# A feature-interaction network on one core: where fc's columns come from, the dummy products of the start, and the queues that load W0 and W1

## The chip, the cores and the metric

The kernel runs on one core of a Trainium2 chip. A core has a matrix engine (TensorE, PE in the profile), a vector engine (VectorE, DVE), a scalar engine (ScalarE, ACT), a general engine (GpSimd, POOL) and an engine that mostly starts transfers (SyncE, SP). Transfers are started from the queues of SP, ACT and POOL, and sixteen DMA engines carry them out. The metric is the device time of one execution in microseconds (us); lower is better. Three runs of the kernel before took 737.26, 740.76 and 745.29 us, median 740.76.

## The reference

The input `x` holds 1,024 samples, 39 fields and 64 values each, in float32. Three layers follow each other, each a sum over all products of a field of the layer's input with a field of `x`:

```python
F, E, HID = 39, 64, [64, 64, 64]
def _cin_layer(Xk, X0, W, b):
    Wr = W.reshape(O, Hk, Fdim)
    return jnp.einsum('bhe,bfe,ohf->boe', Xk, X0, Wr) + b[None, :, None]
Xk = X0
for W, b in ((W0, b0), (W1, b1), (W2, b2)):
    Xk = _cin_layer(Xk, X0, W, b)
    outs.append(Xk.sum(axis=-1))
return jnp.concatenate(outs, axis=-1) @ fc_w.T + fc_b
```

`fc_w` is one row of 192 numbers, 64 for each layer. The result is one number per sample.

## The kernel before, in words

The last step takes only sums over the 64 values and a weighted sum over the channels. So the kernel folds layers 2 and 3 and the output row into weights once, at its start, and then does the two products that remain over all samples.

**The start (the `prep` part, the first 20 us).** From W2 and the third part of `fc_w` it makes V2, a 64 x 39 matrix (line 400, tile `pv`; two DVE transposes at line 417; copies into tile `v2`, lines 427 and 428). The second part of `fc_w` becomes the fortieth column of V2 (`v2[..., F:FT]`, line 424). W0 is transposed on PE (line 411, `pw`) and copied into the upper half of `both` (line 448). V2 times W1 (line 452, tiles `pt` and `pv`) is copied into `part` (line 463), transposed on PE (line 472) and copied into the lower half of `both` (line 481). From `both`, small additions on DVE and copies on ACT (`weight_rows`, lines 498 and 500) make `pairs`, weights for products of two fields, which PE turns into `wa` (`weight_turn`, lines 517 to 519), chunk by chunk.

**The fc columns.** `fc_w` comes as a row into one partition (`fcrow`, line 243, SP). A column of 64 numbers, one a partition, is made on PE as a product of the row with the number one (line 351, `turn_row`, five of them; line 353 for the third part, which is needed twice with a mask by the parity of the partition, lines 311, 332 to 335 and 356). They lie in the PSUM bank `small` and are copied by ACT to `v2` (line 424), `fc` and `fc0s` (lines 645 to 647).

**Dummies.** `spin` (line 277) issues products of ones into the bank `idle`; nobody reads it. Every float32 product shows as two records in the profile.

**The table of products.** Fields are gathered by index from DRAM tables: `gather_rows` (line 171) on POOL fills the tiles `rt`, `ut`, `vt`. The first gathers read `xh`, two transposed pieces of `x` that ACT's queue loads (line 247); SP copies `xh` into the table `xd` (line 390), which later gathers read. DVE multiplies two gathered tiles (`product`, line 211), PE multiplies the result with `wa` (`multiply`, line 533, and `join`, lines 553 and 564), ACT and DVE finish (lines 581, 583, 594).

**Order.** The order on each engine is the program's own, written by hand. The first loads are issued on ACT's queue one behind another: W2, the first `xh`, W0's two halves (line 253), W1's two halves (line 257), the second `xh`. [...]

**The main loop.** 32 blocks of 2,048 columns, in pairs: 13 chunks a pair, each four products of 128 x 512 on PE, save the seventh, which `join` takes.

Of the kernel before, what the change touches and what calls it, by code (L numbers as in the profile page):

```python
# [75 lines left out]
MM = 512  # L76
# [4 lines left out]
NW = 20  # L81
# [63 lines left out]
def cin_kernel(ctx: ExitStack, tc: tile.TileContext, x, w0t, b0, w1, b1, w2, b2, fc_w, fc_b, out):  # L145
    nc = tc.nc
# [13 lines left out]
    def bank(name):  # L160
        return psum.tile([128, MM], F32, name=name, tag="po")
# [43 lines left out]
    def product(n, c, cols=slice(0, BLK), p=None):  # L205
        if p is None:
            p = prods.tile([128, BLK], F32, name="p", tag="p")
        if c < NPAIR:
            i, k = PAIRS[c]
            r = rt[n % 2]  # L210
            nc.vector.tensor_tensor(p[:, cols], r[:, i, cols], r[:, k, cols], ALU.mult)  # L211
        else:
            nc.vector.tensor_tensor(p[:, 0:SUB], ut[n // 2 % 2], vt[n // 2 % 2], ALU.mult)  # L213
        return p

    prep = tc.tile_pool(name="prep", bufs=1)
    with prep as prep:
        w2s = prep.tile([128, FH // 2], F32, name="w2s")
        w1s = prep.tile([128, FH // 2], F32, name="w1s")
        w0s = prep.tile([128, NW * H], F32, name="w0s")  # L220
        part = prep.tile([FT, 4 * NA, H], F32, name="part")
        fcrow = prep.tile([1, 3 * H], F32, name="fcrow")
        fcrow2 = prep.tile([1, H, 2], F32, name="fcrow2")
# [9 lines left out]
        parity = prep.tile([128, 2], I32, name="parity")  # L233
        mask = prep.tile([128, 2], F32, name="mask")

        nc.vector.memset(ones, 1.0)
        nc.vector.memset(fc2, 0.0)
        nc.vector.memset(v2, 0.0)  # L240
        nc.vector.memset(warm, 0.0)
        w0v = w0t.rearrange("b a h -> b (a h)")
        nc.sync.dma_start(fcrow, fc_w)
        nc.scalar.dma_start(w2s, w2.rearrange("o (s n) -> (o s) n", s=2))

        def load_half(k):
            nc.scalar.dma_start(
                xh[k].rearrange("f (b e) -> b f e", e=E), x[k * SB : (k + 1) * SB]
            )

        load_half(0)
        for s, n in enumerate((NW, F - NW)):
            nc.scalar.dma_start(
                w0s[H * s : H * s + F, 0 : n * H], w0v[:, s * NW * H : (s * NW + n) * H]
            )
        for s in range(2):
            nc.scalar.dma_start(
                w1s[H * s : H * s + H], w1[:, s * FH // 2 : (s + 1) * FH // 2]
            )
        load_half(1)  # L260
        nc.gpsimd.iota(place, pattern=[[0, 1]], base=0, channel_multiplier=1)
        for i in range(NT):
            at = OFFSET[i] - 3 * K + (0 if i < NT - 1 else -F)
# [10 lines left out]
        small = bank("small")  # L274


        def spin(n=1, cols=MM // 2):
            for _ in range(n):
                nc.tensor.matmul(  # L279
                    idle[:, 0:cols],  # L280
                    nc.const_aps.tensor(1.0, (128, 128), F32),
                    nc.const_aps.tensor(1.0, (128, cols), F32),
                    start=True,
                    stop=True,
                )

        spin(3)
        spin(1, MM // 4)


# [17 lines left out]

        row, j, f0, late, v, extra = (new() for _ in range(6))
        nc.vector.tensor_copy(row, place)  # L310
        nc.vector.tensor_scalar(parity[:, 1:2], place, 1, None, ALU.bitwise_and)
# [17 lines left out]
        nc.vector.tensor_copy(lists[:, 0:NT], fields_of)  # L329
        nc.vector.tensor_scalar(lists[:, NT : 2 * NT], fields_of, float(FT), None, ALU.add)  # L330

        nc.gpsimd.tensor_copy(mask[:, 1:2], parity[:, 1:2])
        nc.gpsimd.tensor_scalar(mask[:, 0:1], mask[:, 1:2], -1.0, 1.0, ALU.mult, ALU.add)
        for s in range(2):
            nc.gpsimd.tensor_copy(fcrow2[:, :, s], fcrow[:, 2 * H : 3 * H])

        for k, series in enumerate((U_STEPS, V_STEPS)):
            for i, (at, by) in enumerate(series):
                nc.gpsimd.memset(steps_at[:, k, i : i + 1], float(at))
# [5 lines left out]
            nc.gpsimd.dma_start(xd[k][F::FT].rearrange("r (p c) -> p r c", c=128), ones)  # L345


        one = ones[0:1, 0, 0:1]

        def turn_row(dst, k):  # L350
            nc.tensor.matmul(dst, fcrow[:, k * H : k * H + H], one, start=True, stop=True)

        nc.tensor.matmul(
            small[:, 0:1], fcrow2.rearrange("p h s -> p (h s)"), one, start=True, stop=True
        )
        nc.vector.tensor_scalar(fc2[:, 0::32], mask, small[:, 0:1], None, ALU.mult)
        nc.vector.tensor_scalar(unit, apart, 0, None, ALU.is_equal)
        for k in range(3):
            turn_row(small[0:H, k + 1 : k + 2], k)
        for k in range(2):  # L360
            turn_row(small[H:128, k + 4 : k + 5], k)
        spin()


        r, most, seat, far = (new() for _ in range(4))
        both_of = prep.tile([128, 2], F32, name="both_of")
# [30 lines left out]
        for k in range(2):  # L397
            for u in range(2):
# [5 lines left out]
                    start=True,  # L404
                    stop=True,
                )

        for s in range(2):
            for k in range(NW // 2):
                n = min(128, (F - NW * s) * H - k * 128)  # L410
                nc.tensor.transpose(  # L411
                    pw[s][0:n, k * FT : k * FT + F],
                    w0s[H * s : H * s + F, k * 128 : k * 128 + n],
                    unit[H * s : H * s + F, H * s : H * s + F],
                )
# [6 lines left out]
        for s, at in enumerate((2, 5)):  # L422
            rows = slice(H * s, H * s + H)
            nc.scalar.copy(v2[rows, s, F:FT], small[rows, at : at + 1])
# [26 lines left out]
        for k, a in groups:  # L451
# [4 lines left out]
                start=True,  # L456
                stop=True,
# [19 lines left out]
        for k, a in groups:  # L477
            for t in range(2):
                lo = max(NA * k, a + NQ * t)
                n = a + NQ * t + NQ - lo  # L480
# [1 line left out]
                    both[H:128, lo * FT : (lo + n) * FT],  # L482
                    turns[k][H * t : H * t + H, (NQ - n) * FT : NQ * FT],
                )
        spin(4)
        first = [prods.tile([128, BLK], F32, name="p", tag="p") for _ in range(3)]


# [140 lines left out]
    p = {}  # L629
    for k, (n, c) in enumerate(steps[:3]):  # L630
# [28 lines left out]
    for at, (n, c) in enumerate(steps[:-TAIL]):  # L659
# [26 lines left out]
        if at + AHEAD < len(steps):  # L686
            n, c = steps[at + AHEAD]
# [70 lines left out]
```

## Time and profile before

The profiled execution took 737.11 us; its span from the first instruction to the last is 735.3 us.

| what | value |
|---|---|
| median of three runs | 740.76 us |
| profiled execution, span | 737.11 us, 735.3 us |
| PE busy | 729.6 us |
| main products, line 533: 1,536 records | 665.3 us, 593 ns each |
| table products, DVE line 211: 197 | 433.9 us, 2,236 ns each |
| gathers into r, POOL line 171: 156 | 327.1 us, 2,097 ns each |
| dummies, line 279: 22 records | 7.4 us, 484 ns each |
| first record of line 533 | at 19.83 us |

A line of the timeline shows start, busy time, engine, source line, operation, result and inputs, shape and number of records; in brackets stands the idle time before it and what ended it. PE records overlap, so that a record's own duration is longer than the distance to the next. POOL's times are rough.

### The profile page before, as it was taken

The numbers are of one execution on the slowest core, as the hardware profiler recorded it, in microseconds if no ns is written. First come the engines' busy times: TensorE is split into PE (matmuls) and PEld (weight loads), VectorE is DVE, ScalarE is ACT, GpSimd is POOL, SyncE is SP. The second block draws the span as 40 slices with busy tenths as digits, with TensorE's granted clock in tenths as the row PEclk, the third lists the DMA queues.
The fourth block names the chain that finished last, engine by engine and source line by source line (L and its number), as shares of the span: only waits on it lengthen the run. The fifth ranks groups of instructions, "written<-read, shape, count | busy, mean of one in ns | idle before, by whom it ended". The sixth has DMA issues, their size and how long they took to land.

```text
span 735.3 us, 6438 instructions
## 1 busy us (share of the span) xinstructions
PE 729.6 (99%) x2414; PEld 319.1 (43%) x2414; DVE 640.7 (87%) x521; ACT 167.1 (23%) x244; POOL 406.2 (55%) x256
## 2 busy tenths in 40 slices
PE   9999999999999999999999999999999999999998
PEld 6444344444444444444444444444444444444443
DVE  6987998888889888898888889888899888889885
ACT  3232122221212221122221212222122221212222
POOL 7978698547545465554447545465654457545300
PEclk9999999999999999999999999999999999999999
DMA  9869869988576895767878686795767876566700
GB/s 298 335 227 347 329 247 346 386 320 294 233 275 240 301 353 236 262 242 276 321 282 280 235 284 245 297 363 208 270 251 271 330 286 253 221 251 247 285 1 1
DMA packets 63656, 197.25 MB, mean 268 GB/s; under 512 B 37684, under 2 KB 37733, under 8 KB 43656
## 3 DMA queue, kind: packets, MB, share of 16 engines
q0 software_dynamic: 29040, 186.22, 65.6%
q1 hardware_dynamic: 32894, 8.63, 5.1%
q10 hardware_dynamic: 1690, 1.99, 1.1%
q8 instruction: 19, 0.31, 0.2%
q14 instruction: 13, 0.11, 0.0%
HBM read 196.76 MB, written 10.60 MB: 282 GB/s over the span
## 4 chain that ended last, share of the span: by engine, by line
PE 90%; POOL 4%; DVE 2%; DMA 2%; issue 1%; ACT 0%; DVEq 0%
PE po L533 83%; PE po L553 4%; POOL r L171 3%; PE po L564 2%; DMA r<-xd,lists 1%; DMA b0s<-in_b 1%; DVE g L583 1%; DVE p L211 1%; PE pt L452 0%; PE pv L400 0%; POOL v L171 0%; PE pv L452 0%; PE pw L411 0%; POOL u L171 0%; DVE wide L303 0%
## 5 line engine op out<-in xcount | busy, mean ns | idle before, releaser
L533 PE MATMUL po<-p,wa 128*128 128x512 f32 x1536 | 665.3, 593 | 0.8 <-DVE p L211 0.7
L211 DVE TENSOR_TENSOR p<-r 128x2048 f32<-128x2048 f32 (+2 forms) x197 | 433.9, 2236 | 72.0 <-PE po L533 67.0
L171 POOL DMA_INDIRECT r<-xd,lists x156 | 327.1, 2097 | 267.6 <-issue 262.4
L533 PEld LDWEIGHTS po<-p,wa 128*128 128x128 f32 x1536 | 289.8, 190 | 371.6 <-issue 350.0
L581 ACT ACTIVATE z<-po,fc0s 64x512 f32<-64x512 f32 x128 | 87.4, 683 | 378.7 <-PE po L564 216.3
L583 DVE SCALAR_TENSOR_TENSOR g<-po,b0s,z 64x512 f32<-64x512 f32 x128 | 95.9, 749 | 11.5 <-ACT z L581 5.3
L576 ACT COPY g<-r 39x1024 f32<-39x1024 f32 x64 | 66.7, 1043 | 158.9 <-DVE sums L594 122.2
L594 DVE TENSOR_REDUCE sums<-g 103x16 f32<-103x1024 f32 x62 | 75.6, 1220 | 2.1
L171 POOL DMA_INDIRECT u<-xd,lists x16 | 30.6, 1912 | 4.9 <-issue 4.6
L553 PE MATMUL po<-p,wa 32*64 32x512 f32 x512 | 31.6, 600 | 0.0
L171 POOL DMA_INDIRECT v<-xd,lists x16 | 27.9, 1742 | 4.9 <-issue 4.9
L213 DVE TENSOR_TENSOR p<-u,v 128x1024 f32<-128x1024 f32 x16 | 19.5, 1218 | 0.0
L553 PEld LDWEIGHTS po<-p,wa 32*64 32x64 f32 x512 | 9.4, 131 | 20.2 <-issue 19.4
L564 PE MATMUL po<-u,wa 32*64 32x512 f32 x256 | 17.0, 587 | 0.0
L171 POOL DMA_INDIRECT r<-xh,lists x8 | 7.7, 966 | 2.9 <-issue 2.1
L564 PEld LDWEIGHTS po<-u,wa 32*64 32x64 f32 x256 | 5.7, 132 | 8.0 <-issue 8.0
L279 PE MATMUL idle<-const-float32-1.0 128*128 128x256 f32 (+1 forms) x22 | 7.4, 484 | 0.8 <-PEq L745 0.8
L500 DVE TENSOR_TENSOR pairs<-both 128x2 f32<-128x2 f32 (+27 forms) x59 | 6.1, 172 | 0.4 <-issue 0.3
L279 PEld LDWEIGHTS idle<-const-float32-1.0 128*128 128x128 f32 x22 | 5.2, 254 | 1.6 <-issue 0.7
L518 ACT COPY wa<-tr 128x128 f32<-128x128 f32 x8 | 2.1, 266 | 15.1 <-PE tr L517 15.1
L165 POOL DMA_DIRECT2D xd<-in_x x5 | 5.3, 1077 | 0.0
L517 PE MATMUL tr<-unit,pairs 128*128 128x128 f32 x8 | 2.3, 287 | 0.6 <-ACT wa L519 0.5
(101 smaller groups left out, 62.2 us busy)
## 6 DMA issues: line engine op xcount, KB each, us to landing
xd<-in_x SPq DMA_DIRECT2D x26, 312.0 KB
r<-xd,lists POOLq DMA_INDIRECT x156, 8.9
xd<-in_x POOLq DMA_DIRECT2D x5, 312.0 KB, 6.4
w2s<-in_w ACTq DMA_DIRECT2D x1, 624.0 KB
w1s<-in_w ACTq DMA_DIRECT2D x2, 312.0 KB
xh<-in_x ACTq DMA_DIRECT2D x2, 156.0 KB
xd<-xh SPq DMA_DIRECT2D x2, 156.0 KB
u<-xd,lists POOLq DMA_INDIRECT x16, 10.0
```

The costliest lines, as they stand in the source:

```text
L171: nc.gpsimd.indirect_dma_start(dst, None, table, bass.IndirectOffsetOnAxis(ap=lists[:, k : k + 1], axis=0))
L211: nc.vector.tensor_tensor(p[:, cols], r[:, i, cols], r[:, k, cols], ALU.mult)
L213: nc.vector.tensor_tensor(p[:, 0:SUB], ut[n // 2 % 2], vt[n // 2 % 2], ALU.mult)
L279: nc.tensor.matmul(idle[:, 0:cols], nc.const_aps.tensor(1.0, (128, 128), F32), nc.const_aps.tensor(1.0, (128, cols), F32), start=True, sto ...
L500: nc.vector.tensor_tensor(out, diagonal(a, b, sa, sb), diagonal(b, a, sb, sa), ALU.add)
L533: nc.tensor.matmul(po[n][m], wa[:, c, side : side + 2 * H], p[:, bass.ts(m, MM)], start=n % 2 == 0 and c == 0, stop=n % 2 == 1 and c == NP ...
L553: nc.tensor.matmul(dst[half * H : half * H + H], wa[rows, NPAIR, at : at + H], p[rows, bass.ts(side, MM)], start=t >= 2, stop=t < 2 and ha ...
L564: nc.tensor.matmul(dst[half : half + H], wa[rows, NPAIR + 1, H : 2 * H], ut[n // 2 % 2][rows, bass.ts(side, MM)], start=False, stop=t < 2,)
L576: nc.scalar.copy(gt[H : H + F], rt[n % 2][0:F, 0, bass.ts(m, SUB)])
L581: nc.scalar.activation(z[one], po[n][m][other], AF.Identity, bias=fc0s[other])
L583: return lambda: nc.vector.scalar_tensor_tensor(g[n][m // 2][0:H, at], po[n][m][one], b0s[one], z[one], ALU.add, ALU.mult)
L594: nc.vector.tensor_reduce(sums[:, b_at : b_at + SB], g[n][m // 2].rearrange("p (b e) -> p b e", e=E), AX.X, ALU.add,)
```

## The change

It has four parts.

1. `fcrow`, its products, its mask and the bank `small` go. The columns of `fc_w` come by transfers of SP, each of 64 single words (`fc_column`): two into every other partition of `fc2`, two into `v2`, one of three columns into `fc`, two into `fc0s`.
2. The dummies of the start have 2 x 512, 256 and 128 columns instead of 3 x 256 and 128; the one behind the light products goes; 512 and 256 columns are added between the V2 products and the transposes of W0. In front of the first `weight_turn`, `spin(4)` becomes `spin(2, MM)`, the same number of columns.
3. SP loads the first `xh` and the second halves of W0 and W1; ACT loads W2, the first halves and the second `xh`.
4. The clearing of `fc2` comes first on DVE, since the transfers into it wait for it.

```diff
-        nc.sync.dma_start(fcrow, fc_w)
+        def fc_column(dst, k, n=1):
+            nc.sync.dma_start(dst, fc_w[:, k * H : (k + n) * H].rearrange("o (k h) -> h (o k)", h=H))
...
         nc.scalar.dma_start(w2s, w2.rearrange("o (s n) -> (o s) n", s=2))
-        load_half(0)
-        for s, n in enumerate((NW, F - NW)):
-            nc.scalar.dma_start(
+        for s in range(2):
+            fc_column(fc2[s::2, 32 * s : 32 * s + 1], 2)
+        load_half(0, nc.sync)
+        for s, engine in enumerate((nc.scalar, nc.sync)):
+            n = NW - s
+            engine.dma_start(
                 w0s[H * s : H * s + F, 0 : n * H], w0v[:, s * NW * H : (s * NW + n) * H]
             )
+        for s, engine in enumerate((nc.scalar, nc.sync)):
+            engine.dma_start(w1s[H * s : H * s + H], w1[:, s * FH // 2 : (s + 1) * FH // 2])
+        load_half(1, nc.scalar)
         for s in range(2):
-            nc.scalar.dma_start(
-                w1s[H * s : H * s + H], w1[:, s * FH // 2 : (s + 1) * FH // 2]
-            )
-        load_half(1)
+            fc_column(v2[H * s : H * s + H, s, F:FT], 1)
+        fc_column(fc, 0, 3)
+        for s in range(2):
+            fc_column(fc0s[H * s : H * s + H], 0)
...
-        spin(3)
+        spin(2, MM)
+        spin()
         spin(1, MM // 4)
...
-        nc.gpsimd.tensor_copy(mask[:, 1:2], parity[:, 1:2])
-        nc.gpsimd.tensor_scalar(mask[:, 0:1], mask[:, 1:2], -1.0, 1.0, ALU.mult, ALU.add)
-        for s in range(2):
-            nc.gpsimd.tensor_copy(fcrow2[:, :, s], fcrow[:, 2 * H : 3 * H])
...
-        nc.tensor.matmul(
-            small[:, 0:1], fcrow2.rearrange("p h s -> p (h s)"), one, start=True, stop=True
-        )
-        nc.vector.tensor_scalar(fc2[:, 0::32], mask, small[:, 0:1], None, ALU.mult)
         nc.vector.tensor_scalar(unit, apart, 0, None, ALU.is_equal)
-        for k in range(3):
-            turn_row(small[0:H, k + 1 : k + 2], k)
-        for k in range(2):
-            turn_row(small[H:128, k + 4 : k + 5], k)
-        spin()
...
+        spin(1, MM)
+        spin()
         for s in range(2):
             for k in range(NW // 2):
...
-        spin(4)
+        spin(2, MM)
...
-    nc.scalar.copy(fc, small[0:H, 1:4])
-    nc.scalar.copy(fc0s[0:H], small[0:H, 1:2])
-    nc.scalar.copy(fc0s[H:128], small[H:128, 4:5])
```

More of the change, by code (lines that the diff above doesn't have):

```diff
@@ L221, in cin_kernel @@
         part = prep.tile([FT, 4 * NA, H], F32, name="part")
-        fcrow = prep.tile([1, 3 * H], F32, name="fcrow")
-        fcrow2 = prep.tile([1, H, 2], F32, name="fcrow2")
         fc2 = prep.tile([128, H], F32, name="fc2")
@@ L232, in cin_kernel @@
         lane = prep.tile([128, 1], I32, name="lane")
-        parity = prep.tile([128, 2], I32, name="parity")
-        mask = prep.tile([128, 2], F32, name="mask")
+        nc.vector.memset(fc2, 0.0)
         nc.vector.memset(ones, 1.0)
-        nc.vector.memset(fc2, 0.0)
         nc.vector.memset(v2, 0.0)
@@ L242, in cin_kernel, with load_half @@
         w0v = w0t.rearrange("b a h -> b (a h)")
-        nc.sync.dma_start(fcrow, fc_w)
-        nc.scalar.dma_start(w2s, w2.rearrange("o (s n) -> (o s) n", s=2))
-        def load_half(k):
-            nc.scalar.dma_start(
+        def fc_column(dst, k, n=1):
+            nc.sync.dma_start(dst, fc_w[:, k * H : (k + n) * H].rearrange("o (k h) -> h (o k)", h=H))
+        def load_half(k, engine):
+            engine.dma_start(
                 xh[k].rearrange("f (b e) -> b f e", e=E), x[k * SB : (k + 1) * SB]
             )
-        load_half(0)
-        for s, n in enumerate((NW, F - NW)):
-            nc.scalar.dma_start(
+        nc.scalar.dma_start(w2s, w2.rearrange("o (s n) -> (o s) n", s=2))
+        for s in range(2):
[3 more added lines that the diff above has]
+            n = NW - s
+            engine.dma_start(
                 w0s[H * s : H * s + F, 0 : n * H], w0v[:, s * NW * H : (s * NW + n) * H]
             )
+        for s, engine in enumerate((nc.scalar, nc.sync)):
+            engine.dma_start(w1s[H * s : H * s + H], w1[:, s * FH // 2 : (s + 1) * FH // 2])
+        load_half(1, nc.scalar)
         for s in range(2):
-            nc.scalar.dma_start(
-                w1s[H * s : H * s + H], w1[:, s * FH // 2 : (s + 1) * FH // 2]
-            )
-        load_half(1)
+            fc_column(v2[H * s : H * s + H, s, F:FT], 1)
+        fc_column(fc, 0, 3)
+        for s in range(2):
+            fc_column(fc0s[H * s : H * s + H], 0)
         nc.gpsimd.iota(place, pattern=[[0, 1]], base=0, channel_multiplier=1)
@@ L273, in cin_kernel @@
         pw = [bank("pw") for _ in range(2)]
-        small = bank("small")
         def spin(n=1, cols=MM // 2):
@@ L310, in cin_kernel @@
         nc.vector.tensor_copy(row, place)
-        nc.vector.tensor_scalar(parity[:, 1:2], place, 1, None, ALU.bitwise_and)
         step(row, F, 1.0, j)
@@ L345, in cin_kernel @@
             nc.gpsimd.dma_start(xd[k][F::FT].rearrange("r (p c) -> p r c", c=128), ones)
-        one = ones[0:1, 0, 0:1]
-        def turn_row(dst, k):
-            nc.tensor.matmul(dst, fcrow[:, k * H : k * H + H], one, start=True, stop=True)
-        nc.tensor.matmul(
-            small[:, 0:1], fcrow2.rearrange("p h s -> p (h s)"), one, start=True, stop=True
-        )
-        nc.vector.tensor_scalar(fc2[:, 0::32], mask, small[:, 0:1], None, ALU.mult)
-        nc.vector.tensor_scalar(unit, apart, 0, None, ALU.is_equal)
-        for k in range(3):
-            turn_row(small[0:H, k + 1 : k + 2], k)
-        for k in range(2):
-            turn_row(small[H:128, k + 4 : k + 5], k)
-        spin()
+        nc.vector.tensor_scalar(unit, apart, 0, None, ALU.is_equal)
         r, most, seat, far = (new() for _ in range(4))
@@ L421, in cin_kernel @@
         column = blocks.rearrange("h k (f j) -> h (k f) j", j=32)[:, :, 0]
-        for s, at in enumerate((2, 5)):
-            rows = slice(H * s, H * s + H)
-            nc.scalar.copy(v2[rows, s, F:FT], small[rows, at : at + 1])
         for s in range(2):
```

## The prediction

> **What bounds the kernel now.** I read the page first, then the chain of waits from 60 us on, then the PE, POOL and DVE timelines of the first 45 us.
>
> ```profile
> span 735.3 us, 6438 instructions
> PE 729.6 (99%) x2414; PEld 319.1 (43%) x2414; DVE 640.7 (87%) x521; ACT 167.1 (23%) x244; POOL 406.2 (55%) x256
> ```
>
> PE is hardly ever idle (735.3 - 729.6 = 5.7 us). The chain says from when that is true without a break (start, length, what):
>
> ```profile
> 79.10 2.29 DVE p L211
> 81.39 0.04 issue
> 81.44 7.13 PE po L533 x16
> ...
> 91.33 41.40 PE po L533 x96
> ```
>
> From 81.44 us the chain holds PE pieces alone up to 730.36 us. The change touches none of that: the 653.9 us after 81.44 stay. What it can do is to bring the 81.44 us mark forward or push it back. Two things lead to it. PE's own work is one (main products from 19.83 us on); the other is the table gathers on POOL, whose last members DVE waits for (the chain shows a gather landing from 60.74 to 68.94 us, then DVE, then PE at 81.44).
>
> The PE timeline of the start (start, busy, what):
>
> ```profile
> 0.78 3.33 PE L279 MATMUL idle<-const-float32-1.0 128*128 128x256 f32 x8 [0.78 <-PEq L745]
> ...
> 7.07 2.40 PE L400 MATMUL pv<-w2s,fc 128*64 128x320 f32 x8
> 9.40 1.91 PE L411 MATMUL pw<-unit,w0s 39*128 39x39 f32 x20
> 11.24 2.50 PE L452 MATMUL pt<-w1s,v 128*128 128x320 f32 x4
> 13.54 2.17 PE L452 MATMUL pv<-w1s,v 128*128 128x320 f32 x4
> ...
> 17.08 2.01 PE L279 MATMUL idle<-const-float32-1.0 128*128 128x256 f32 x8
> ```
>
> The reader should divide. The eight L452 records take 11.24 to 15.64 us: 550 ns for 320 columns, 1.72 ns a column. The dummies at 17.08 take (19.03 - 17.08)/8 = 244 ns for 256, 0.95 a column; the main products 41.40/96 = 431 ns for 512, 0.84. So until 15.6 us PE ran at half speed. The page's clock row says 9 and the windows 1.00 throughout: that row does not show this state.
>
> [...] DMA share 0.95 to 1.19 in every microsecond from 3 to 20 us. [...]
>
> ```profile
> 17.70 0.94 POOL L171 DMA_INDIRECT r<-xd,lists  x1 [0.30 <-issue]
> ...
> 23.20 5.27 POOL L171 DMA_INDIRECT r<-xd,lists  x1 [0.30 <-issue]
> ```
>
> and on DVE
>
> ```profile
> 22.90 4.63 DVE L211 TENSOR_TENSOR p<-r 128x1024 f32<-128x1024 f32 x4
> ```
>
> The 5.27 us gather ends at 28.47, 0.94 us after the DVE run ended at 27.53. A gather gets its 0.94 us of work done only between DVE products.
>
> **The change, part by part.**
>
> *Dummies (PE).* 2 x 512 + 256 + 128 columns, two records each, 2,816 column-records at 1.72 ns = 4.8 us: from 0.78 to 5.6 us without a gap, where before the dummies stopped at 4.11. [...]
>
> *V2's input.* W2 was there by 4.83 us (the ACT queue's second xh load waits for that semaphore and is issued then). Now 156 KB of xh run beside it: at the window's 380 GB/s, 0.4 us, so 5.2. The two fc2 words' transfers (64 words each) are issued by SP after a DVE memset at about 1.0 and 1.4 us. The trace has such a transfer only under full load: bias and b0s, 0.2 KB, 4.4 and 4.6 us to landing; fcrow, one row, was in use 1.3 us after issue (0.73 to 2.03). Bounds 2.7 and 6.0; I take 3.5, under the dummies. L400 starts at 5.6 instead of 7.07 and takes 1.2 (released) to 2.3 us. DVE must first end its index lists (7.03 us before, less 0.4 for parity and the fc2 product): its two transposes and copies then run 6.7 to 8.4 (or to 9.2, if L400 is slow), against 8.45 to 10.52. The 768 dummy columns behind L400 (1.5 us at 0.95) end near 8.3, under that cover. The 20 W0 transposes at L472's released rate, 1.44/20 = 72 ns, take 1.4 instead of 1.8: to 9.7.
>
> *L452.* It needs v2 (9.2 at the latest), both halves of W1 and now v2's fc words. In the program's order of waits, the second half of W1 [...]must wait for the semaphore of W2's load: issued at 5.2 instead of 3.64 us. In the trace before, PE's wait for W1 ended at 10.3 us, set by 1.94 MB on busy engines. Those bytes stay, so I take 10.3 again for W1, 0.5 more for the words behind it on SP (bounds: 0 and the 4.6 us of b0s), start 10.8. Eight records of 320 columns at 0.85 ns: 2.2 us instead of 4.4. End 13.0 against 15.64: **2.6 us earlier**. The copies to `part` follow 1 us behind as before (ACT 0.85 us a pair); the rest up to the first product of L533 keeps its length, because `spin(2, MM)` has the same 1,024 columns as `spin(4)`. L533 starts at 17.2 instead of 19.83.
>
> *Costed at nothing.* ACT issues four loads instead of six; its next needed work is at 10.07. Parity, mask and fcrow copies (POOL, 0.83 us) came before the zero rows and gathers; the first gather at 6.47 needs xh (SP saw it at 5.64), so at most 0.8 us is gained and I take 0.3, as xh now stands behind two word transfers but beside W2. ACT's v2, fc and fc0s copies: 0.16 us each, no later ACT work waited. SP's `xd<-xh` copies now stand behind ten transfers and their semaphores (halves of W0 and W1, xh): second one at about 11.5 to 12.3 instead of 10.92. Cover: its reader, the gather at 17.70, and that gather's data are used at 31.35. fc and fc0s are first used at 45.67.
>
> *What is late next.* The second halves of the first gathers land (landing events of the trace) at 20.3, 21.7 and 23.5 us; DVE used them at 24.04, 25.17 and 26.31. The least slack is 2.8 us: 2.6 fits, more would not. Further on, gathers need gaps in DVE's products; the one issued at 37.88 got out at 43.63, behind the DVE gap at 42.83 in which DVE waits for PE to free a buffer. So that gap moves with PE, and the chain to 81.44 with it. Against that, first products starting 2.6 us sooner lock out two or three gathers that were out before. I leave 2.5 us, with 0 to 4.5 as bounds.
>
> **Sum.** 737.1 (profiled execution: span 735.3 and 1.8 around it) - 2.5 = 734.6. The three runs were 737.3, 740.8 and 745.3; with the profiled one the median of four is 739.0, and from there 736.5. That is my forecast for the runs.
>
> **Rivals.**
> (a) *The gathers take it back*: PE starts 2.6 us sooner, but gathers locked out between 15 and 20 us make the 81.44 mark stand. For it: the chain enters PE through DVE and a gather there, and PE idles 0.7 us in front of it. Against it: DMA runs at 0.54 (25 to 30 us) and 0.33 (40 to 45), so there is room to catch up. 739.0.
> (b) *The clock is not released early*: a gap before L400 (W2 after 5.6 us)[...]; then only the 0.4 us of start are won. 738.6.
> (c) *Slower: word transfers.* SP serves words, xh, halves of W0 and W1 in one line with semaphore waits. If v2's words land after 13.4 us (10.8 + 2.6), L452 starts so late that the released clock no longer pays. At two successive b0s-like landings (5.8 + 2 x 4.6 = 15.0) it ends at 17.2, 1.6 us late: 740.6; with the xd copies pushed likewise, 742.
> (d) *It does more*: W1 and words land by 9.2, L452 ends at 11.4, and the gathers keep up: 4.2 us, 734.8.
>
> **Chances.** Forecast 0.45, (a) 0.2, (b) 0.1, (c) 0.15, (d) 0.1. A measurement of this kernel can tell about 1%, 7.4 us, from no change. No case reaches that by itself; only the scatter of runs (8 us over three) can: faster 0.06, same 0.88, slower 0.06. The range, 732.5 to 742.5, holds the bounds 0 and 4.5 of the gain, (c), and about 2 us of scatter on each side.
>
> **What would show it.** Right: L452's records near 270 ns each and L533 first at about 17 us; 44.16 us per pair of blocks unchanged; the mark of 81.44 at about 79. Wrong: L452 still at 550 ns (b); PE waiting on v2 or W1 past 13 us (c); L533 early but PE idle between 40 and 82 us (a).

## The result, and the profile after

| | before | changed | ratio, 95% interval |
|---|---|---|---|
| first measurement, 22 runs each (set 1) | 738.07 us (734.42 to 745.29) | 743.68 us (739.04 to 747.04) | 1.0073 [1.005, 1.0096] |
| profiled execution, span | 737.11, 735.3 us | 742.79, 741.0 us | |

The change made the kernel 5.6 us slower; the forecast was 736.5 us, 2.5 less than before. The loss is under the 1% that the forecast counted as a difference, but it has the other sign and lies outside the range. Five later sets of runs followed, each on one chip of its own. Four of them (sets 3 to 6) ran the changed kernel again and gave 1.0019 to 1.0076 (below). In what follows a set's kernels are compared with each other and with the kernel before in the same set. The ratios are estimates over the fast executions (one of e15, 746.97 us, was slow and is left out) and differ by up to 0.0017 from the quotient of two medians.

The page of the changed kernel begins:

```profile
span 741.0 us, 6410 instructions
PE 730.7 (99%) x2400; PEld 317.7 (43%) x2400; DVE 640.7 (86%) x519; ACT 166.5 (22%) x239; POOL 387.6 (52%) x252
```

PE works 1.1 us more than before and idles 10.3 us instead of 5.7. The timeline of PE's start (start, busy, what; in brackets the idle time before it and what ended it):

```profile
0.79 4.62 PE L282 MATMUL idle<-const-float32-1.0 128*128 128x512 f32 x8 [0.79 <-PEq L724]
7.84 2.07 PE L383 MATMUL pv<-w2s,fc 128*64 128x320 f32 x8 [2.42 <-DMA fc<-in_fc_w]
9.84 2.46 PE L282 MATMUL idle<-const-float32-1.0 128*128 128x512 f32 x4
12.23 1.19 PE L396 MATMUL pw<-unit,w0s 39*128 39x39 f32 x20
13.35 1.43 PE L434 MATMUL pt<-w1s,v 128*128 128x320 f32 x4
14.61 1.32 PE L434 MATMUL pv<-w1s,v 128*128 128x320 f32 x4
18.11 1.03 PE L454 MATMUL pw<-unit,part 40*128 40x40 f32 x10 [2.17 <-DVE part L445]
19.13 1.29 PE L454 MATMUL pt<-unit,part 40*128 40x40 f32 x10
20.34 3.78 PE L282 MATMUL idle<-const-float32-1.0 128*128 128x512 f32 x4
...
26.72 1.12 PE L515 MATMUL po<-p,wa 128*128 128x512 f32 x2 [1.18 <-issue]
```

and the first main product of the kernel before:

```profile
19.83 1.02 PE L533 MATMUL po<-p,wa 128*128 128x512 f32 x2
```

Line 383 is V2 (before: 400), 434 is V2 times W1 (452), 454 the transposes of `part` (472), 515 the main products (533). Three things are to be seen. PE waits 2.42 us for the two columns of `fc2`, which before were there in time. The 768 dummy columns behind V2 stand with their 2.46 us in front of the W0 transposes, which start at 12.23 instead of 9.40. And the V2 x W1 records do start about 290 ns apart instead of 530 (the forecast: near 270 instead of 550), but 2.17 us of waiting and 3.78 us for 1,024 dummy columns (2.0 before) follow, so that the first main product comes at 26.72 instead of 19.83.

The granted clock in stretches (each line: the stretch, its length, busy time and instructions of five engines, then PEclk, DMA share, GB/s):

```profile
0.00:5.00 5.00, 4.21 (x6) 2.08 (x7) 3.89 (x25) 1.47 (x2) 4.21 (x46) 1.00 0.56 154
5.00:10.00 5.00, 2.58 (x12) 1.06 (x11) 2.05 (x15) 0.00 (x0) 0.00 (x0) 0.83 0.92 240
...
20.00:25.00 5.00, 5.00 (x12) 2.52 (x12) 2.87 (x18) 1.48 (x5) 3.42 (x4) 0.50 1.03 404
```

The clock falls back twice. The trace's clock records put it at full from 4.86 us, half from 8.28, full from 11.69, half from 18.52 and full from 25.34 us on; before, it was full from 15.38 us on without a break. This also corrects the prediction, which said that the clock row does not show this state: it shows it from the first record on, and the kernel before had none until 15.38.

POOL's first gather, before and after:

```profile
6.47 1.06 POOL L171 DMA_INDIRECT r<-xh,lists  x1 [0.73 <-DVE tmp L378]
```

```profile
10.29 1.03 POOL L171 DMA_INDIRECT r<-xh,lists  x1 [5.43 <-DMA xh<-in_x]
```

`xh` now lands at 9.44 us instead of 5.62. From 28.93 us on the chain of waits holds PE alone (but for 0.4 us of ACT's copies at 46.1), 44.16 us a pair of blocks as before. The `join` products of the second pair, before and after:

```profile
90.27 1.06 PE L564 MATMUL po<-u,wa 32*64 32x512 f32 x16
```

```profile
95.82 1.06 PE L546 MATMUL po<-u,wa 32*64 32x512 f32 x16
```

They start 5.55 us later, and the span is 5.7 longer. So the loss lies in the start.

### The profile page after: what moved, and what is told of

It reads as the page before. It is cut to its first block, busy times and chain, and to the rows that moved or that the text cites. A ratio compares the mean times of both kernels' runs of the same rounds, so it can differ in the third digit from the quotient of the medians.

```text
span 741.0 us, 6410 instructions
## 1 busy us (share of the span) xinstructions
PE 730.7 (99%) x2400; PEld 317.7 (43%) x2400; DVE 640.7 (86%) x519; ACT 166.5 (22%) x239; POOL 387.6 (52%) x252
## 4 chain that ended last, share of the span: by engine, by line
PE 97%; DVE 1%; DMA 1%; issue 0%; ACT 0%; DVEq 0%; SPq 0%
PE po L515 89%; PE po L535 4%; PE po L546 2%; DMA fc<-in_fc_w 1%; DVE p L211 0%; DVE pairs L482 0%; PE idle L282 0%; PE pv L434 0%; PE pv L383 0%; PE pt L454 0%; PE pt L434 0%; PE pw L396 0%; PE pw L454 0%; DVE part L445 0%; PE tr L499 0%
## 5 line engine op out<-in xcount | busy, mean ns | idle before, releaser
L171 POOL DMA_INDIRECT r<-xd,lists x156 | 304.9, 1955 | 286.7 <-issue 275.1
L171 POOL DMA_INDIRECT u<-xd,lists x16 | 33.4, 2086 | 5.3 <-issue 5.3
L171 POOL DMA_INDIRECT v<-xd,lists x16 | 29.5, 1842 | 4.9 <-issue 4.9
L282 PE MATMUL idle<-const-float32-1.0 128*128 128x512 f32 (+2 forms) x20 | 12.3, 771 | 0.8 <-PEq L724 0.8
L383 PE MATMUL pv<-w2s,fc 128*64 128x320 f32 x8 | 2.1, 651 | 2.4 <-DMA fc<-in_fc_w 2.4
```

The costliest lines, as they stand in the source:

```text
L171: nc.gpsimd.indirect_dma_start(dst, None, table, bass.IndirectOffsetOnAxis(ap=lists[:, k : k + 1], axis=0))
L282: nc.tensor.matmul(idle[:, 0:cols], nc.const_aps.tensor(1.0, (128, 128), F32), nc.const_aps.tensor(1.0, (128, cols), F32), start=True, sto ...
```

## The experiments

The theory after the first profile: the single-word transfers are late and hold V2 and the first `xh`, and the idle time that they make costs the clock. Rivals: the added dummies, which stand in front of the W0 transposes; and the two queues.

**Set 2: one part of the change undone.**

e1 gives all words back to the row, the light products, the mask and ACT's copies (and DVE its old order of clearing); new dummies and queues stay. The lines that bring the products, the mask and the copies back are left out here.

```diff
+        nc.sync.dma_start(fcrow, fc_w)
...
-        for s in range(2):
-            fc_column(fc2[s::2, 32 * s : 32 * s + 1], 2)
...
-        for s in range(2):
-            fc_column(v2[H * s : H * s + H, s, F:FT], 1)
-        fc_column(fc, 0, 3)
-        for s in range(2):
-            fc_column(fc0s[H * s : H * s + H], 0)
```

> The changed kernel with fc's columns made on PE again from a row, as before; its dummies and its two queues stay. Theory A (the single words hold up V2: the two transfers into fc2 landed at 5.83 and 7.71 us, and PE waited 2.42 us for them; the words also hold up xh behind them on SP): V2's first product starts at 5.5 to 6.5 us, its first gather on POOL at about 6, time 3 to 6 us below the changed kernel, ratio to before 0.995 to 1.003. Theory B (the dummies cost, not the words: 768 columns stand between V2 and the transposes of W0 at half clock): ratio stays near 1.007. Theory C (the queue split delays xh through sharing with W2): first gather stays near 10 us, ratio near 1.007.

e2 gives back the dummies of before (and the one behind the light products), e3 the queues of before, with the words left on SP:

```diff
 # e2
-        spin(2, MM)
-        spin()
+        spin(3)
...
+        spin()
...
-        spin(1, MM)
-        spin()
...
-        spin(2, MM)
+        spin(4)
 # e3
-        load_half(0, nc.sync)
-        for s, engine in enumerate((nc.scalar, nc.sync)):
+        load_half(0, nc.scalar)
+        for s in range(2):
...
-            engine.dma_start(
+            nc.scalar.dma_start(
...
-        for s, engine in enumerate((nc.scalar, nc.sync)):
-            engine.dma_start(w1s[H * s : H * s + H], w1[:, s * FH // 2 : (s + 1) * FH // 2])
+        for s in range(2):
+            nc.scalar.dma_start(w1s[H * s : H * s + H], w1[:, s * FH // 2 : (s + 1) * FH // 2])
```

> The changed kernel with the dummies of before (3 x 256 and 128 at the start, 256 ahead of V2, none between V2 and the transposes, 4 x 256 at the end). Theory A: V2 still starts at 7.8 us after fc2's words; without the 768 columns the transposes of W0 start at about 10 instead of 12.2 us, so up to 2 us are won, but the clock is released later; ratio to before 1.003 to 1.008. Theory B: ratio 1.000 to 1.002. Theory C: 1.007.

> The changed kernel with all loads of W2, xh, W0, W1 on ACT's queue in the old order; SP carries the words alone. Theory A: fc2's words still wait beside W2's packets and land at 5 to 8 us, V2 still late, ratio 1.003 to 1.007; the first gather on POOL goes back to about 6.5 us. Theory C: first gather 6.5 us and the ratio falls to 1.000 to 1.002. Theory B: 1.007.

e4 puts the first `xh` ahead of `fc2`'s words on SP:

```diff
+        load_half(0, nc.sync)
         for s in range(2):
             fc_column(fc2[s::2, 32 * s : 32 * s + 1], 2)
-        load_half(0, nc.sync)
```

> The changed kernel with xh's first load ahead of fc2's words on SP; nothing else. It tells whether the late gathers (first one 10.29 instead of 6.47 us) set the end. Theory A in its narrow form (V2's words set the end, the gathers have slack): first gather 6 to 7 us, V2 at 8 us or later, ratio 1.006 to 1.010. Theory C (late gathers set the end): ratio 1.000 to 1.003.

Before, in this set: 735.58 us. Ratios come from 6 to 14 executions, the times behind them from one profiled execution each. Those of e1 and e2 were the slowest of their kernels (738.86 and 740.45 us at medians of 736.11 and 737.38), so their times of the start are late ones.

| | ratio, interval | V2 | first gather | V2 x W1 | first main product |
|---|---|---|---|---|---|
| e1 words back | 1.0007 [0.9996, 1.0019] | 7.39 | 8.29 | 14.04 | 20.74 |
| e2 dummies back | 1.0025 [1.0016, 1.0033] | 7.92 | 10.46 | 12.60 | 24.49 |
| e3 queues back | 1.0098 [1.0082, 1.0113] | 5.81 | 6.42 | 15.84 | 23.79 |
| e4 `xh` first | 1.003 [1.0014, 1.0046] | 9.77 | 7.35 | 15.25 | 21.81 |

Without words the loss is gone. Without the new dummies it stays: the changed kernel itself was not in this set, but stands at 1.0019 to 1.0033 in sets 3, 4 and 6. In e4 the first gather is nearly back at its old time and V2 waits for the words until 9.77 us instead; the loss is still 1.003. The chain of waits of e4 leads from the second word transfer (2.15 to 9.63 us) into V2 and on along PE. So a late `xh` is not needed for a loss; late words in front of V2 do as well.

e3 is instructive: with `xh` on ACT, the words land at 5.04 and 5.67 us, inside the prediction's bounds, V2 starts close to its 5.6 us, and the kernel is the slowest of all. The PE timeline and POOL's:

```profile
15.84 2.47 PE L434 MATMUL pt<-w1s,v 128*128 128x320 f32 x4 [5.71 <-DMA w1s<-in_w]
```

```profile
6.42 1.03 POOL L171 DMA_INDIRECT r<-xh,lists  x1 [1.57 <-DVE both_of L363]
...
21.45 0.98 POOL L171 DMA_INDIRECT r<-xh,lists  x1 [9.15 <-DMA xh<-in_x]
```

With the words on SP, ACT issues its loads of W1 at 6.30 and 6.86 us (before: 3.08 and 3.64), though the same four loads stand ahead of them on its queue. The early gathers are now issued before the second of them: W1 lands at 15.7 us, the second `xh` lets the gather at 21.45 go. What holds ACT's issue in e3 was not shown. In set 1 an issue that uses nothing of W2 comes right behind W2's last landing event: before, ACT's second `xh` at 4.83 us behind 4.81; in the changed kernel, SP's second half of W1 at 4.76 behind 4.75 (forecast: 5.2).

**Set 3: the words moved, the queues alone, `fc2` alone.** e5 is the changed kernel once more. e6 puts `fc2`'s words on ACT's queue ahead of W2 and the first `xh` first on SP:

```diff
-        nc.scalar.dma_start(w2s, w2.rearrange("o (s n) -> (o s) n", s=2))
         for s in range(2):
-            fc_column(fc2[s::2, 32 * s : 32 * s + 1], 2)
+            fc_column(fc2[s::2, 32 * s : 32 * s + 1], 2, 1, nc.scalar)
+        nc.scalar.dma_start(w2s, w2.rearrange("o (s n) -> (o s) n", s=2))
```

e7 is the kernel before with the two queues alone. e8 is the changed kernel with `fc2` alone from the row (one light product and the mask, as before).

> The changed kernel once more. In its profile DVE and ACT start to copy V2 times W1 at 17.06 and 17.31 us, 2.9 us after PE's records of the first of these products end, and PE runs cold from 18.5 to 25.3 us. If that gap belongs to the kernel (theory: PE waits for something that the records do not show), it comes again in place and size, ratio 1.006 to 1.009. If it belongs to that execution alone, the copies start within 0.2 us of the products and the first main product comes 2 us sooner or more.

> The words of fc2 are issued on ACT's queue ahead of W2; xh is first on SP as in the run with xh first. If the words were late because they stood behind W2's large packets, they land at 3 to 4 us here (9.63 in the run with xh first) and V2 starts as soon as W2 is there, at 6 to 7.5 us; ratio to before 0.997 to 1.002. If single words are slow by themselves, they land after 5 us, W2 after 7, ratio 1.002 to 1.006.

> The kernel before with nothing but the split of xh, W0 and W1 over two queues. Theory: the sixteen engines are shared, so that nothing comes sooner, and xh, which now runs beside W2 and W0, comes at 7 to 7.5 us instead of 5.6, so the first gather starts at about 8.2 instead of 6.5. If that does not set the end: ratio 0.999 to 1.001. If it does: 1.001 to 1.003.

> The changed kernel with fc2 alone made from the row on PE; the words for v2, fc and fc0s stay on SP behind W1. If the early words (fc2) are the loss: ratio 0.999 to 1.002, as with all words taken back. If the late ones are: 1.004 to 1.007.

Before, in this set: 735.38 us.

| | ratio, interval | V2 | first gather | V2 x W1 | first main product |
|---|---|---|---|---|---|
| e5 changed kernel | 1.0025 [1.0012, 1.0037] | 7.84 | 10.08 | 13.33 | 19.92 |
| e6 words ahead | 1.0059 [1.0046, 1.0072] | 9.31 | 5.15 | 14.74 | 21.30 |
| e7 queues alone | 1.0004 [0.9995, 1.0014] | 6.27 | 7.85 | 10.31 | 18.53 |
| e8 `fc2` from the row | 1.0025 [1.0013, 1.0037] | 6.15 | 8.12 | 12.06 | 20.22 |

e6 says where the words stood. Issued ahead of W2, the two transfers land at 3.89 and 4.85 us instead of 7.42 and 9.63 (e4). But V2 gains little on e4 and loses on e5, since W2 now lands at 9.2 instead of about 5. Part of this is the order of issue: ACT issues W2 behind the two words at 2.39 us instead of 0.75, and its first packet is carried at 3.81 instead of 1.78, when `xh` on SP has already begun. PE's timeline:

```profile
9.31 2.40 PE L383 MATMUL pv<-w2s,fc 128*64 128x320 f32 x8 [3.49 <-DMA w2s<-in_w]
```

The trace's transfer records of the profiled execution of set 1, counted by half microseconds from 2.5 to 7.5 us:

```
                                2.5 3.0 3.5 4.0 4.5 5.0 5.5 6.0 6.5 7.0
ACT's queue, 4992 B (W2, W0)     28  39  32   3   0   1  10  25  19   7
SP's queue, 4 B                    0   0   0  47  16  26  32  29   9   4
SP's queue, 256 B (first xh)      0   0   0   0   0   0   0   5 104 240
```

(The 4 B packets are the 128 words and some that belong to no word: the row's transfer in e1 has one too.) SP issued the words at 0.97 and 1.64 us, yet none is carried before 4.09, when W2's packets have run out, and `xh`, next on the same queue, starts at 6.19, when the words are nearly through. In e1, where one row of 768 B takes the place of the words, that single packet is carried at 1.65 us, before the first of W2 (1.78), and `xh`'s packets begin at 3.77 us. In e6, where W2 is not yet on its way, `xh`'s packets begin at 2.20 us. So in the changed kernel SP's words and `xh` were carried only when all but 3 of W2's 128 packets (from 1.79 us on) had begun, and the words then took another 2 us of `xh`'s time. They need not always take that long: in e3, beside the 256 B packets of `xh` on ACT's queue, SP's 4 B packets were 570 by 6.0 us; here, beside 5,120 B packets of W0, 121. That the packets beside them are the reason was not tested.

e8 shows the other group of words. V2 starts at 6.15, but V2 x W1 waits for `v2`'s words, and then it runs at half clock (half from 11.90 to 15.31 us):

```profile
12.06 2.47 PE L451 MATMUL pt<-w1s,v 128*128 128x320 f32 x4 [1.93 <-DMA v<-in_fc_w]
```

So the words behind `fc2`'s are enough for the loss (e8 and e5 have the same ratio). Whether `fc2`'s two are enough by themselves this set does not show; e14 below does not settle it. And e5's profile lacks what made set 1 worse, the 2.17 us of waiting behind V2 x W1 and the second stretch at half clock.

**Set 4: the clock, and the dummies by themselves.** e9 adds two dummies of 512 columns behind those of the start of the changed kernel, to fill the 2.4 us. e10 is the kernel before with the new dummies alone. e11 is the kernel before with one dummy of 256 columns between its first light product and the others. e12 is the changed kernel a third time.

```diff
 # e9
         spin(1, MM // 4)
+        spin(2, MM)
 # e11
         nc.vector.tensor_scalar(unit, apart, 0, None, ALU.is_equal)
+        spin()
```

> The changed kernel with two more dummies of 512 columns behind those of the start (four records, 1.7 us at the released clock, 3.5 us at half), so that PE has little idle time between the dummies and the V2 products at about 7.8 us. Theory 'idle throws the clock back': the clock is released by 7.6 us and stays released; the 768 dummies in front of the W0 transposes take 1.3 us instead of 2.4 to 2.9, the V2 x W1 products start at about 12 us instead of 13.3, the main products 1.3 us sooner than in the changed kernel, ratio to before about 1.000 to 1.001. Rival 'the words' lateness alone': V2 and what follows are held by the words and by W1; the main products start where they did (19.9 or later), ratio 1.0025 as for the changed kernel.

> The kernel before with only the dummies of the change (fc's row and light products, and all loads on ACT's queue, as before). Theory 'the words are the loss': no loss from this part; the 768 dummies cost some 1.4 to 2.9 us in front of the W0 transposes and the warm V2 x W1 products give 1 to 2.2 back, ratio 0.999 to 1.001. Rival 'the 768 dummies are the loss': main products start 1.5 us or more after those of before (19.83), ratio 1.002 or more.

> The kernel before with one more dummy of 256 columns between its first light product and the five others; nothing else. A candidate to beat both kernels. Theory 'a gapless start is what releases the clock': PE has no gap over 0.3 us from 0.8 to 9.4 us, the clock is released by 7.6 us, the V2 x W1 records come near 290 ns apart instead of 550, the main products start near 17.8 instead of 19.83, ratio 0.997 to 0.998. Rival 'W1 and the gathers hold the start': the records are short but the gathers set the mark at 81 us; ratio 0.999 to 1.0005.

> The changed kernel, unchanged, a third time. If the 1.0073 of the first measurement belongs to the kernel, it comes again, with the 2.9 us between the V2 x W1 products and the copies to part and with a second half-clock stretch from 18.5 to 25.3 us. If it depends on how the clock's windows fall in an execution, the ratio stands near 1.0025 and these stretches are not in the profile.

Before, in this set: 735.33 us. "First join" is the start of the first `join` products on the short tiles, line 546 or its like.

| | ratio, interval | full clock from | first gather | V2 x W1 | first main product | first join |
|---|---|---|---|---|---|---|
| before (profile of set 1) | | 15.38 | 6.47 | 11.24 | 19.83 | 44.61 |
| e9 bridge | 1.0026 [1.0012, 1.004] | 6.66, held | 10.42 | 12.50 | 19.52 | 45.67 |
| e10 dummies alone | 0.9986 [0.997, 1.0002] | 5.88, held | 6.65 | 10.93 | 17.61 | 42.38 |
| e11 row bridge | 0.9994 [0.9985, 1.0003] | 4.99, lost 11.82 to 22.06 | 6.28 | 10.59 | 21.43 | 45.68 |
| e12 changed kernel | 1.0033 [1.0023, 1.0043] | 5.64, lost 9.06 to 12.47 | 10.42 | 13.50 | 20.06 | 45.70 |

e9 takes half of the theory away. The clock is held (PE waits 0.18 us in front of V2 instead of 2.21), V2 x W1 comes 1.0 us sooner than in e12, the main products 0.5, and the first join and the time stay. DVE's timeline and the chain of waits of e9 name what holds it (start, length, what):

```profile
18.68 0.69 DVE L211 TENSOR_TENSOR p<-r 128x512 f32<-128x512 f32 x1 [0.60 <-DMA r<-xh,lists]
```

```profile
19.12 1.06 POOL r L171
...
20.49 7.18 DMA r<-xh,lists
...
27.69 1.22 DVE p L211
```

The first gather comes 3.95 us later than before, and the gathers' data come last. Further back the chain goes the same way in e9, e5 and e12; e12's:

```profile
2.25 7.32 DMA xh<-in_x
...
9.59 0.65 SPq L241
...
10.28 0.61 SPq L241
...
10.93 0.59 SPq L241
...
11.57 0.86 SPq L373
...
12.49 6.38 DMA xd<-xh
```

It goes from the late `xh` through SP's three last word transfers (line 241: `fc` and `fc0s`, which nobody needs before 45 us) to SP's copies of `xh` into the table, then to a gather that waits for them, DVE and PE. In these executions the words cost through `xh` and SP's line, not through the clock.

It is not the only path. In set 1, where the clock was lost twice, and in e13 and e16 of the sets below, the chain of the same kernel leads from the second word transfer into V2 and from there along PE. Set 1's:

```profile
1.64 6.07 DMA fc<-in_fc_w
...
7.84 2.07 PE pv L383 x8
```

e10 is the part of the change that the prediction had right. The clock is full from 5.88 us, the first main product comes 2.2 us sooner than before, the first join too. Then, in the chain of waits of e10:

```profile
77.75 2.29 DVE p L211
...
80.09 7.13 PE po L534 x16
```

The mark that stood at 81.44 stands at 80.09: of 2.2 us 1.35 are left, and PE waits 1.59 us for DVE in front of it instead of 0.71. The median is 1.3 us less than before, with an interval that touches 1. e11, meant to beat both, lost its clock again (10.24 us at half) in the gap before W1 and shows no difference.

**Sets 5 and 6: does the larger loss come again, and which words make it?** e13 and e16 are the changed kernel, e15 is e10 again and e17 e1 again. e14 keeps only `fc2`'s words and takes the rest from the row; e18 keeps `fc2`'s and `v2`'s words and takes only `fc` and `fc0s` from the row.

```diff
 # e14
-        for s in range(2):
-            fc_column(v2[H * s : H * s + H, s, F:FT], 1)
-        fc_column(fc, 0, 3)
-        for s in range(2):
-            fc_column(fc0s[H * s : H * s + H], 0)
+        nc.sync.dma_start(fcrow, fc_w)
...
+        for k in range(3):
+            turn_row(small[0:H, k + 1 : k + 2], k)
+        for k in range(2):
+            turn_row(small[H:128, k + 4 : k + 5], k)
```

The five light products stand behind the 768 dummies; ACT copies them as before.

> The changed kernel, unchanged, on a further chip. Theory 'the single words cost about 2 us, the rest of the first measurement's loss is that chip's': ratio 1.002 to 1.004 and no gap of over 1 us between the V2 x W1 products and the copies to part. Rival 'the kernel has two ways to run, and either can come': ratio 1.005 or more, or runs near 737.5 and near 743 side by side.

> The changed kernel with only fc2's two columns by single words; v2's, fc's and fc0s's columns come from the row by five light products, behind the 768 dummies, and ACT copies. Theory 'either group of words costs': the two words of fc2 alone still hold V2 to about 7.8 us and the first xh to about 9.4, so that the first gather is issued near 10.3 and the ratio stays at 1.002 to 1.003. Rival 'the late words hold the V2 x W1 products': those start 0.5 us or more sooner than in the changed kernel, the main products too, ratio 1.0005 or less.

> The kernel before with only the dummies of the change, a second time and on another chip. Theory 'the dummies by themselves give half of what the prediction gave the whole change (2.5 us)': main products start near 17.6 us instead of 19.83, ratio 0.998 to 0.9995, interval below 1. Rival 'the first result was scatter': ratio 1.000 or more.

> The changed kernel, unchanged, beside the next two on one chip. It tells which kind of chip this is: ratio near 1.003 with the part copies right behind the V2 x W1 products, or near 1.0075 with some 3 us between them.

> The changed kernel without any single word (row, light products, mask and ACT copies as before; dummies and queues of the change), a second time. Theory 'the words are the loss on every chip': within 0.2% of before, whatever the changed kernel does beside it. Rival 'on the worse kind of chip the new dummies or the queues lose too': ratio 1.003 or more where the changed kernel stands at 1.005 or more.

> The changed kernel with only fc's and fc0s's columns (320 single words, first used at 45 us) from the row; fc2's and v2's stay single words. Theory 'the words that are needed at the start cost': V2 at 7.8 us, first gather near 10.3, ratio as the changed kernel's within 0.0015. Rival 'the 320 late words, whose packets run from 12 to 18 us, disturb the stretch in which V2 x W1 is copied': the gap there goes, main products 2 us or more sooner than in the changed kernel where that has the gap; no difference where it has none.

| | set, before | median | ratio, interval |
|---|---|---|---|
| e13 changed kernel | 5, 738.25 | 745.10 | 1.0076 [1.0056, 1.0097] |
| e14 only `fc2` by words | 5 | 738.92 | 1.001 [0.9979, 1.0041] |
| e15 dummies alone | 5 | 736.71 | 0.9962 [0.9936, 0.9989] |
| e16 changed kernel | 6, 735.47 | 737.65 | 1.0019 [1.0008, 1.003] |
| e17 words back | 6 | 735.64 | 0.9994 [0.998, 1.0008] |
| e18 `fc`, `fc0s` from the row | 6 | 738.14 | 1.0042 [1.0031, 1.0054] |

The larger loss came again. In sets 1 and 5 the kernel before takes 738 us and the changed one 744 to 745, in sets 3, 4 and 6 they take 735.4 and 737.6. Most of the difference goes with the granted clock, which is on record for every execution. (What came before the first release did not count in it: the profile of the kernel before has 1.0, though its release came at 15.38 us.) The changed kernel spent 12 and 13 us at half clock in sets 1 and 5, 2.6 to 3.2 in the others, means over all executions. In the profiles of set 1 the V2 x W1 records start 530 ns apart ahead of the release and 290 at full clock, so half clock loses up to about half of its time, and these 10 us more can be, as an estimate from that, up to 5 of the 6 to 7.5 us more. On set 5's chip the kernel before took 735.26 us (median) in the 15 executions that kept the clock, about as elsewhere, and 738.5 to 745.2 in the 25 at 0.995 or less. Each chip of sets 2 to 6 was measured once, and that of set 1 is not on record, so whether the chip makes the difference is not shown.

The profiles differ at one handover. ACT's timeline of e13 and of e12, the copy of W0's transposes (line 430), whose last PE record starts at 13.13 and 13.37 us:

```profile
16.47 0.94 ACT L430 COPY both<-pw 64x390 f32<-64x390 f32 x2 [5.41 <-PE pv L434]
```

```profile
13.61 0.94 ACT L430 COPY both<-pw 64x390 f32<-64x390 f32 x2 [3.02 <-PE pw L396]
```

In e12 ACT starts 0.24 us after PE's last record has started, in e13 3.34 us. In set 1 it was 3.14, in e14 2.5 and in e15, which has no word at all, 2.2; in e5, e10 and e16 0.23 to 0.24; in the kernel before of set 1, at half clock, 0.30. So this delay does not need the words; all three kernels of set 5 have it, and e4, e9, e17 and e18 of other sets (0.24 to 0.29 us) have not. In e13 PE waits behind it and half clock follows, from 18.22 to 31.87 us; in e15, where the rest of the start is earlier, the clock stays full until 68 us. What delays the handover no record shows, and it stays open.

e14 on such a chip is 6.2 us below e13, and the two start alike (V2 7.75 and 7.77, first gather 10.44 and 10.39). Its interval, 0.9979 to 1.0041, holds both no loss and 2 us, so it does not tell what `fc2`'s words cost alone. e14's half-clock stretch ends at 22.24 instead of 31.87. Whether `v2`'s 128 words or the 320 behind them make the difference there was to be told by e18; it ran where the loss was small, and taking the 320 away helped nothing: 1.0042 is above e16's 1.0019 (its profiled execution, 741.13 us at a median of 738.14, had half clock from 7.38 to 21.04 us). That stays open too.

## Why the prediction was wrong, and where it was right

*Dummies.* Right in most executions: the clock was released at 4.86 us instead of 15.38, and V2 x W1 took 290 ns a record (forecast: near 270). That longer dummies would bring the release forward was the author's estimate, which the trace of before, with its one release, did not show; e10, with the new dummies alone, has it at 5.88 us. It is partly luck: in the profiles of e16 and e1, with the same dummies, the release came only at 13.63 and 13.46 us, which is rival (b). In the kernel where this part stands alone (e10) the first main product came at 17.61 us; the prediction had 17.2. The size was too large: the sum let the gathers follow for 2.5 us, and they followed for 1.35 of 2.2, so that rival (a) took back 0.9 us by the 81 us mark. Measured alone: 0.9986, with an interval that touches 1, and 0.9962.

*V2's input: this step failed.* The prediction put the words at 3.5 us, bounds 2.7 and 6.0, "under the dummies"; they landed at 5.83 and 7.71. The upper bound is an issue at 1.4 us and the 4.6 us that b0s took to land; the second transfer was issued at 1.64 and took 6.07. The value taken lies near fcrow's 1.3 us, but fcrow is one packet, carried before W2's first (1.64 and 1.78 us). The records show that SP's words waited until W2's packets on ACT's queue were nearly through (none before 4.09 us), a wait for which the prediction had no term; what makes them wait no run shows. In set 1 the chain of waits runs through the second transfer into V2: this is where the first microseconds were lost.

*The first gather ("at most 0.8 us is gained and I take 0.3"): this step failed with it.* `xh` was said to stand "behind two word transfers but beside W2". It waited for them in full: 9.44 us instead of 5.62, the first gather 3.8 us later. In e5, e9 and e12 the chain of waits runs through `xh` and the gathers, and holding the clock (e9) does not help; in set 1, e13, e16 and e4 it runs through V2, in e8 through `v2`'s words. e1 and e17, without words, are at 1.0007 and 0.9994: that the words are the loss is shown, the share of each path is not. (In the profiles the second join of e17 lies only 0.57 us before that of e12, at 89.81 and 90.38; e17's profiled execution was 1.0 us above its median.)

*"Costed at nothing": SP's copies into the table.* The time was right (11.4 and 12.4 us; forecast 11.5 to 12.3 for the second), the cover was not: in e12 the copy issued at 12.49 lands at 18.86 us, after the 17.70 at which its reader was issued before, and in e5 and e12 it is on the chain of waits.

*The queues.* No gain was counted and none came (e7: 1.0004). But with two queues at work the first `xh` lands later even without words: at 7.0 (e7) and 8.5 us (e17) instead of 5.6. e17, which is e10 with the two queues, has the same first main product, 17.61 us, and its first join at 45.13 instead of 42.38, its second at 89.81 instead of 88.92. So in these profiles the queues take back part of what the dummies give, and the prediction had no term for it; the intervals of the two ratios overlap.

*Not forecast: the clock lost again.* The prediction treated the release as lasting. It was lost over a wait of 2.0 to 2.5 us in front of V2 in set 1, e5, e12 and e13, and kept in e9, which fills that wait (0.18 us are left). In the records all stretches between two changes are multiples of 3.41 us (at half clock 3.41 in e8, 10.24 in e11, 13.65 in e13), and their phase differs between executions of one kernel (full from 4.86, 5.91, 5.64, 4.57 and 13.63 us in the five profiles of the changed kernel). Laid on a grid of such windows of 3.41 us, all profiles of the case agree (the last 2 us of a span left out): a window at full clock in which PE idled less than 1.1 us never lost it, one with more than 1.6 us always did, and between the two both occur (17 losses, at 1.16 to 3.41 us).

*Rival (c)* had the sign and the kind of cause, and SP's line with its copies pushed back. But it looked at `v2`'s words in front of V2 x W1 (after 13.4 us), while in set 1 PE waited for `fc2`'s words in front of V2. Its 740.6 to 742 would have been nearer than the forecast. The larger loss of sets 1 and 5 was no case of the prediction's. The range, too, was too narrow by its own words: 742.5 leaves 0.5 us above (c)'s 742, not the 2 us of scatter.

## What to carry to other kernels

A transfer of single words can land late when large loads are under way (4.9 and 6.1 us after issue here); count the landing of everything behind it on its queue, not only its own. A released TensorE clock is only worth what the next wait leaves of it (1.16 us of idle time in a 3.41 us window was enough to lose it in e7), and a faster PE only what the gathers behind it can follow (1.35 of 2.2 us in e10). Where a start-up change gains or loses some 2 us of 735, repeat it on several chips and look at the granted clock of each execution before a size is believed.

## What was not expected of the hardware

- The same kernel took 737.5 us in some sets and 745 in another, along with 3 or 13 us at half clock; and at one handover ACT starts 0.24 us or 2.2 to 3.3 us after PE's last record has started.
- The clock fell to half over waits of 1.16 us (e7) and more between busy stretches, and in e13 a later half-clock stretch lasted 13.65 us.
- Putting a transfer earlier moved the loss instead of removing it: words ahead of W2 landed 3.5 and 4.8 us sooner, and W2 4 us later, of which its later issue is 1.6 us.
